# A graph layer with a mixture of experts: expert steps in multiples of 16 rows, and another list of steps

## The chip, the cores and the metric

The kernel runs on one core of a Trainium2 chip. The metric is the device time of one launch, the median over several runs: 1311.78 us before the change (three runs, 1311.54 to 1311.91). TensorE multiplies, VectorE (DVE) and ScalarE (ACT) work on vectors, GpSimd (POOL) issues the indirect transfers, and SyncE (SP) issues nearly all other transfers.

## The reference

For 6250 nodes of 256 features and 106250 edges (100000 random ones and a loop per node, sorted by target), the reference computes a graph convolution and then a feed-forward layer with 8 experts, of which each node uses its best two:

```python
deg = maximum(segment_sum(ones, dst), 1); norm = deg ** -0.5
y = norm * (layernorm(x) @ W.T + b)
x = x + norm * segment_sum(y[src], dst)                  # sum over the edges
g = layernorm(x)
p, idx = top_k(g @ Wg.T + bg, 2); p = softmax(p)
for e in range(8):                                       # W1[e]: 1024 x 256, W2[e]: 256 x 1024
    out += combine[..., e] * (relu(g @ W1[e].T + b1[e]) @ W2[e].T + b2[e])
x = x + out
```

All of it is float32. The kernel computes an expert only for the rows that chose it: 2 x 6250 = 12500 rows over the eight experts.

## The kernel before, in words

The kernel is one program with an order written out by hand. It has four parts.

**Start.** Node degrees are counted, the nodes are normalised, and a table with one row per node is written to memory (`ftable`).

**The stream.** The edges lie in 831 chunks of 128. For each chunk, called a slot here, POOL issues one indirect transfer that gathers 128 rows of the table (`gather`, L459), DVE makes a mask, and TensorE multiplies mask and rows into a window of sums (`add_up`, L473). The gather runs 6 slots ahead in the order of the program and has 24 buffers. When the edges of a tile of 128 nodes are all in, the tile goes through a chain of small tasks that are planned by slot: its sums are joined, multiplied by W (L566), normalised, scored, its two experts found, its rows sorted by expert (L698) and sent to a queue per expert in memory (`fhq`, L721, eight transfers on SP's queue).

**Expert steps.** The rows in the queues are worked off in steps. One step takes up to a fixed number of rows of one expert. `choose` (L730 and on) picks on DVE the expert with the most waiting rows at that moment. Then SP loads the expert's W1 (`load_first`, L773, 1152 KB), the rows (`load_rows`, L781) and W2 (`load_second`, L786, 1028 KB); each weight has three buffers, so W1 of a step is loaded when at most two steps ahead of it have not finished their up half, and W2 likewise by finished steps. TensorE works in pieces. An *up* piece (L814) computes 128 of the 1024 hidden values: two float32 matmuls, which the profile shows as four records, whose moving operand has as many columns as the step has rows. ACT applies bias and relu (L816). A *down* piece (L824) multiplies two of the eight blocks of hidden values by W2, for 128 rows of the step: again four records, with 256 columns. So a step has 8 up pieces, and 4 down pieces for each half of 128 rows. Up pieces of one step alternate with down pieces of the step before. When a half is complete, DVE adds the bias (L836) and SP writes the result to memory (`fyq`, L838).

How many rows a step has, and from which slot its choice may be made, is in the list STREAM (52 steps); nine further steps (TAIL) are chosen behind the stream, when all rows are sent. In every slot TensorE's order is filled by a credit: 1250 ns per slot, less 225 for the slot's own matmul and the planned tasks, and pieces are issued as long as credit is left:

```python
credit = min(credit + SLOT - CHUNK - busy.get(s, 0), SPARE)
while credit > 0:
    ...
    kind = next_piece(s)
    if not kind: break
    credit -= PIECES[ROWS_OF[of[kind == "down"]]][kind == "down"]
```

Pieces that are left when the slots run out follow one by one (the tail), together with the chains of the last tiles.

**End.** Each node's two results are read back by indirect transfers on POOL's queue (`read_back`, L907, 98 of them), weighed and added (L915), and the output is stored (L922). The list DONE says which tiles may be read back after which step: a pair (step, tile) means that all rows of tiles below `tile` lie in steps up to `step`. Before a group is read, `results` (L902) makes its addresses on DVE. If a tile's rows should lie in a later step than DONE says, or rows be left over, a flag is set, and a second, slower way of computing everything is entered (`any_order`).

Of the kernel before, what the change touches and what calls it, by code (L numbers as in the profile page):

```python
# [19 lines left out]
P = 128  # L20
N = 6250
NT = 49
# [12 lines left out]
CAP = 27 * FT  # L35
QR = NE * CAP
SLOTS = 64
STREAM = ((58, 128), (64, 128), (70, 128), (89, 128), (125, 256), (131, 256), (154, 256), (169, 256),
          (184, 256), (199, 256), (214, 256), (230, 256), (247, 256), (264, 256), (281, 256), (293, 256),
          (310, 256), (325, 256), (341, 256), (355, 256), (371, 256), (386, 256), (401, 256), (417, 256),  # L40
          (433, 256), (450, 256), (467, 256), (484, 256), (501, 256), (518, 256), (535, 256), (553, 256),
          (570, 256), (587, 256), (604, 256), (621, 256), (633, 256), (650, 256), (665, 128), (673, 256),
          (689, 256), (705, 256), (720, 256), (735, 128), (744, 256), (760, 256), (775, 256), (790, 256),
          (806, 256), (821, 128), (829, 128), (838, 128))
TAIL = (256, 256, 256, 256, 256, 256, 128, 128, 128)
ROWS_OF = [n for s, n in STREAM] + list(TAIL)
USUAL = len(ROWS_OF)
START = [P + sum(ROWS_OF[:step]) for step in range(USUAL + 1)]


# [1 line left out]
CHUNK = 225  # L52
SPARE = 2000
TASKS = dict(turn_sum=220, linear=890, rank=100, sort=430, inputs_turned=800, inputs_scored=1570)
PIECES = {FT: (915, 870), P: (600, 870)}
W1C = 2 * H + HB
W2C = HB * D + D

# [7 lines left out]
GROUP = 7  # L66
SHIFT = 1.0 / 16

DONE = ((36, 26), (38, 28), (40, 29), (41, 30), (42, 31), (43, 32), (46, 35), (49, 37), (50, 38), (51, 39),
        (52, 41), (55, 42), (57, 43), (58, 44), (59, 48), (USUAL - 1, NT))  # L70
LATER = 1 << 17
TURNED, PLACED, SORTED, SENT = 5, 17, 22, 24
LEAD = (13, 12)
# [73 lines left out]
def in_order(ctx: ExitStack, tc: tile.TileContext, g: Shared):  # L147
# [670 lines left out]
    def down(step, i, s):  # L818
        f = steps[step]
        a = i // 4  # L820
        if i % 4 == 0:
            f["py"] = psp.tile([P, D], F32, name="py")
        for b in (2 * (i % 4), 2 * (i % 4) + 1):
            nc.tensor.matmul(f["py"], f["hid"][:, b, a * P:(a + 1) * P], f["w2"][:, b * D:(b + 1) * D],  # L824
                             start=(b == 0), stop=(b == HB - 1))
        if i % 4 == 3:
            plan_at(s + 1, leave, step, a, f["py"], f["w2"])
        if i == 4 * ROWS_OF[step] // P - 1:
            del steps[step]


    def leave(step, a, py, w2):

        nonlocal gone
        y = work.tile([P, D], F32, name="y", bufs=4)
        nc.vector.tensor_add(y, py, w2[:, HB * D:])  # L836
        r0 = START[step] + a * P
        w = nc.sync.dma_start(yq[r0:r0 + P, :], y)  # L838
        free_order(w, reads, "results are written once, and read once written")
        writes.append((step, w))  # L840
        if a == ROWS_OF[step] // P - 1:
            gone += 1


# [91 lines left out]
    def next_piece(s):  # L936

        nonlocal curu, curd, done, upped, was
        was = next_kind(s)
        if was == "up":  # L940
            up(upped, curu)
            curu += 1
            if curu == HB:
                upped, curu = upped + 1, 0
        if was == "down":
            down(done, curd, s)
            curd += 1
            if curd == 4 * ROWS_OF[done] // P:
                done, curd = done + 1, 0
        return was  # L950

    with tc.manual_schedule():
        with rowp as rowpool:
# [5 lines left out]
            for s in range(NC):  # L959
# [8 lines left out]
                while credit > 0:  # L968
                    of = upped, done
                    kind = next_piece(s)  # L970
                    if not kind:
                        break
                    credit -= PIECES[ROWS_OF[of[kind == "down"]]][kind == "down"]
        with tc.tile_pool(name="ftail", bufs=2) as pool:
            s = NC
            pend = []
# [568 lines left out]
```

## Time and profile before

| | |
|---|---|
| median of the runs | 1311.78 us |
| the profiled execution | 1585.69 us |
| its span, first to last instruction | 1583.8 us |
| mean granted TensorE clock | 0.896 |
| first and last matmul of a slot (L473) | 76.9 and 1365.3 us |
| read-backs | 98 x 0.965 us on POOL |
| last TensorE piece ends, last instruction ends | about 1561.7 and 1583.8 us |

The profile is of one execution, recorded by the hardware, and it takes 274 us longer than the runs that are timed. A row of its groups names line, engine, operation and operands, then the number of instructions, the busy time and the mean duration of one, then the idle time ahead of it and what ended it. The duration of a matmul holds the time in which its results drain; the next one has begun by then, so the price of a piece is the distance from start to start. The row of stages gives, for a stretch of time, the busy time of each engine, the granted clock, the share of the DMA engines that was busy, and the rate of bytes.

### The profile page before, as it was taken

What the parts mean: (1) busy time and instruction counts of PE and PEld (TensorE: products, weight loads), DVE (VectorE), ACT (ScalarE), POOL (GpSimd) and SP (SyncE); (2) the same over time, 40 slices, a digit from 0 to 9 for tenths busy, and PEclk for the clock granted to TensorE, in tenths of its full rate; (3) what the DMA queues carried; (4) which work ended last, traced back from release to release, by engine and by line L of the source; (5) the groups of instructions that cost most, each with busy time, mean ns of one, the idle gap of its engine ahead of it and who ended that gap; (6) DMA issues with size and microseconds to landing.
All of it is one profiled execution on the core that took longest, in us unless ns stands there. A gap on an engine that the chain in (4) does not pass through costs nothing.

```text
span 1583.8 us, 24462 instructions
## 1 busy us (share of the span) xinstructions
PE 1255.9 (79%) x6400; PEld 953.5 (60%) x6400; DVE 980.3 (62%) x5472; ACT 397.4 (25%) x949; POOL 904.2 (57%) x975
## 2 busy tenths in 40 slices
PE   5239678479889888898988787888889888777894
PEld 5226566256666566666666565666666666665783
DVE  8611665565667676776766676767766676574632
ACT  3502222122222222222222222232222222221221
POOL 2166656556666566565666666656666664236633
PEclk9955678789999999899899999999999999888997
DMA  7633485577767676767767776767867767678863
GB/s 230 209 93 91 117 273 167 133 232 224 234 207 222 205 246 219 232 183 241 216 216 217 226 228 206 229 202 219 270 216 239 245 210 231 197 232 304 312 229 119
DMA packets 160925, 337.35 MB, mean 213 GB/s; under 512 B 26900, under 2 KB 106344, under 8 KB 145160
## 3 DMA queue, kind: packets, MB, share of 16 engines
q1 hardware_dynamic: 114348, 207.57, 37.7%
q0 software_dynamic: 46176, 127.59, 28.9%
q8 instruction: 52, 0.85, 0.2%
q14 instruction: 97, 0.79, 0.2%
q10 hardware_dynamic: 252, 0.53, 0.1%
HBM read 280.44 MB, written 55.16 MB: 212 GB/s over the span
## 4 chain that ended last, share of the span: by engine, by line
PE 60%; DVE 17%; issue 10%; another core or an unknown queue 6%; ACT 2%; DMA 2%; POOL 1%; SPq 1%; ACTq 0%; DVEq 0%; POOLq 0%
PE ph L814 22%; PE py L824 18%; PE ps L473 10%; PE pt L566 3%; PE ph L516 2%; DVE mask L466 2%; PE px L698 2%; PE count L291 1%; ACT hid L816 1%; DVE rolled L533 1%; PE px L505 1%; DVE rs L595 1%; DVE rolled L536 1%; DVE scr L750 1%
## 5 line engine op out<-in xcount | busy, mean ns | idle before, releaser
L459 POOL DMA_INDIRECT rows<-ftable,src x831 | 789.4, 950 | 508.6 <-PE ps L473 187.4
L814 PE MATMUL ph<-xT,w 128*128 128x256 f32 (+1 forms) x1952 | 515.4, 392 | 115.0 <-issue 65.3
L814 PEld LDWEIGHTS ph<-xT,w 128*128 128x128 f32 x1952 | 366.0, 203 | 236.9 <-issue 107.6
L824 PE MATMUL py<-w,hid 128*128 128x256 f32 x1760 | 468.9, 393 | 0.0
L816 ACT ACTIVATE hid<-ph,w 128x256 f32<-128x256 f32 (+1 forms) x488 | 216.9, 451 | 791.5 <-PE ps L473 260.6
L824 PEld LDWEIGHTS py<-w,hid 128*128 128x128 f32 x1760 | 340.8, 197 | 76.9 <-issue 2.7
L473 PE MATMUL ps<-rows,mask 128*128 128x512 f16 x831 | 327.4, 409 | 38.8 <-DMA rows<-ftable,src 28.3
L466 DVE TENSOR_SCALAR mask<-col_b,rel 128x128 f16<-128x128 bf16 x831 | 199.1, 266 | 32.5 <-issue 11.6
L907 POOL DMA_INDIRECT yb<-fyq,rowat x98 | 94.6, 965 | 113.7 <-DMA fyq<-y 54.0
L473 PEld LDWEIGHTS <-mask 128*128 128x128 f16 x831 | 88.1, 107 | 71.8 <-issue 32.2
L836 DVE TENSOR_TENSOR y<-py,w 128x256 f32<-128x256 f32 x110 | 46.4, 422 | 134.4 <-PE py L824 61.8
L533 DVE SCALAR_TENSOR_TENSOR rolled<-rolled,keep,ps 128x256 f32<-128x256 f32 x149 | 70.7, 474 | 44.7 <-PE ps L473 34.5
L573 DVE SCALAR_TENSOR_TENSOR xr<-pt,norm,xr 128x256 f32<-128x256 f32 x49 | 23.7, 483 | 118.8 <-PE ps L473 55.2
L548 ACT ACTIVATE whole<-rolled 32x256 f32<-32x256 f32 (+2 forms) x156 | 63.8, 409 | 59.8 <-DVE rolled L536 26.6
L516 PE MATMUL ph<-wg,turned 128*128 128x8 f32 x196 | 39.9, 332 | 48.2 <-issue 26.5
L516 PEld LDWEIGHTS ph<-wg,turned 128*128 128x128 f32 x196 | 38.7, 291 | 62.4 <-issue 33.7
L536 DVE TENSOR_TENSOR rolled<-ps,rolled 128x256 f32<-128x256 f32 x150 | 63.6, 424 | 15.8 <-DVE rolled L533 7.2
L566 PE MATMUL pt<-gw,uT 128*128 128x264 f32 x196 | 58.3, 424 | 18.3 <-issue 7.2
L698 PE MATMUL px<-slots,h2s 128*128 128x256 f16 x196 | 33.1, 297 | 37.2 <-DVE slots L686 20.4
L915 DVE SCALAR_TENSOR_TENSOR xr<-yb,prob,xr 128x256 f32<-128x256 f32 x98 | 46.0, 482 | 25.3 <-DMA yb<-fyq,rowat 23.2
L566 PEld LDWEIGHTS pt<-gw,uT 128*128 128x128 f32 x196 | 40.0, 209 | 34.6 <-issue 19.8
L698 PEld LDWEIGHTS <-h2s 128*128 128x128 f16 x196 | 20.5, 105 | 54.1 <-issue 42.4
(184 smaller groups left out, 1127.1 us busy)
## 6 DMA issues: line engine op xcount, KB each, us to landing
w<-in_W SPq DMA_DIRECT2D x61, 1152.0 KB
w<-in_W SPq DMA_DIRECT2D x61, 1028.0 KB
fhq<-ordered SPq DMA_DIRECT2D x392, 64.0 KB
fyq<-y SPq DMA_DIRECT2D x110, 128.0 KB
rows<-ftable,src POOLq DMA_INDIRECT x831
xT<-fhq SPq DMA_DIRECT2D x49, 256.0 KB
out<-xr POOLq DMA_DIRECT2D x11, 512.0 KB
xr<-in_x SPq DMA_DIRECT2D x6, 896.0 KB
```

The costliest lines, as they stand in the source:

```text
L459: nc.gpsimd.indirect_dma_start(out=rows[c], out_offset=None, in_=table[:, :], in_offset=bass.IndirectOffsetOnAxis(ap=g.src[:, c:c + 1], ax ...
L466: nc.vector.tensor_scalar(masks[c], g.col_b[:, r:r + P], g.rel[:, c:c + 1], None, op0=OP.is_equal)
L473: nc.tensor.matmul(sums[w], masks.pop(c), rows.pop(c), start=(c == chunks[0]), stop=(c == chunks[-1]))
L516: nc.tensor.matmul(px[:, t - t0], xT[:, k, (t - t0) * P:(t - t0 + 1) * P], wg[:, k, :], start=(k == 0), stop=(k == 1))
L533: nc.vector.scalar_tensor_tensor(new, rolled, keeps[kept[w]], ps[:, 0:D], op0=OP.mult, op1=OP.add)
L536: nc.vector.tensor_add(new, ps[:, D:2 * D], new)
L566: nc.tensor.matmul(pl, uT[:, k, :], gw[:, k, :], start=(k == 0), stop=(k == 1))
L698: nc.tensor.matmul(r.px[:, k, :], h2s[r.t][:, i, k * P:(k + 1) * P], slots[r.t], start=(i == 0), stop=(i == 1))
L814: nc.tensor.matmul(ph[:, :n], w1[:, k * H + b * P:k * H + (b + 1) * P], f["xT"][:, :n, k], start=(k == 0), stop=(k == 1))
L816: nc.scalar.activation(f["hid"][:, b, :n], ph[:, :n], AF.Relu, bias=w1[:, 2 * H + b:2 * H + b + 1])
L824: nc.tensor.matmul(f["py"], f["hid"][:, b, a * P:(a + 1) * P], f["w2"][:, b * D:(b + 1) * D], start=(b == 0), stop=(b == HB - 1))
L907: r = nc.gpsimd.indirect_dma_start(out=yb, out_offset=None, in_=yq[0:START[upto + 1], :], in_offset=bass.IndirectOffsetOnAxis(ap=where[:, ...
```

## The change

Steps may have any multiple of 16 rows up to 256. A half of a step that isn't full has `m` rows instead of 128, in the matmuls of the down pieces, in the bias add and in the write. An up piece is priced by its columns, 29 ns for eight of them and at least 300 ns, instead of by a table with two entries: 928 instead of 915 ns for 256 rows, 464 instead of 600 for 128. The list STREAM has 53 entries instead of 52: five steps of 128 rows and one of 208, then 37 of 256, then ten of 128 rows from slot 762 to 844. TAIL has eight steps of falling size instead of nine. DONE is another list, for the new steps. The lines of the diff:

```diff
--- before.py
+++ after.py
@@ -35,16 +35,17 @@
 CAP = 27 * FT
 QR = NE * CAP
 SLOTS = 64
-STREAM = ((58, 128), (64, 128), (70, 128), (89, 128), (125, 256), (131, 256), (154, 256), (169, 256),
-          (184, 256), (199, 256), (214, 256), (230, 256), (247, 256), (264, 256), (281, 256), (293, 256),
-          (310, 256), (325, 256), (341, 256), (355, 256), (371, 256), (386, 256), (401, 256), (417, 256),
-          (433, 256), (450, 256), (467, 256), (484, 256), (501, 256), (518, 256), (535, 256), (553, 256),
-          (570, 256), (587, 256), (604, 256), (621, 256), (633, 256), (650, 256), (665, 128), (673, 256),
-          (689, 256), (705, 256), (720, 256), (735, 128), (744, 256), (760, 256), (775, 256), (790, 256),
-          (806, 256), (821, 128), (829, 128), (838, 128))
-TAIL = (256, 256, 256, 256, 256, 256, 128, 128, 128)
+STREAM = ((74, 128), (91, 128), (99, 128), (108, 128), (118, 128), (126, 208), (175, 256), (183, 256),
+          (206, 256), (222, 256), (237, 256), (253, 256), (268, 256), (284, 256), (300, 256), (316, 256),
+          (332, 256), (348, 256), (365, 256), (380, 256), (395, 256), (411, 256), (427, 256), (450, 256),
+          (467, 256), (480, 256), (497, 256), (513, 256), (529, 256), (545, 256), (560, 256), (575, 256),
+          (591, 256), (607, 256), (623, 256), (638, 256), (655, 256), (672, 256), (686, 256), (702, 256),
+          (719, 256), (737, 256), (754, 256), (762, 128), (771, 128), (784, 128), (796, 128), (804, 128),
+          (812, 128), (820, 128), (828, 128), (836, 128), (844, 128))
+TAIL = (256, 224, 208, 208, 176, 160, 144, 128)
 ROWS_OF = [n for s, n in STREAM] + list(TAIL)
 USUAL = len(ROWS_OF)
+HALVES = [-(-n // P) for n in ROWS_OF]
 START = [P + sum(ROWS_OF[:step]) for step in range(USUAL + 1)]
 
 
@@ -52,7 +53,7 @@
 CHUNK = 225
 SPARE = 2000
 TASKS = dict(turn_sum=220, linear=890, rank=100, sort=430, inputs_turned=800, inputs_scored=1570)
-PIECES = {FT: (915, 870), P: (600, 870)}
+DOWN = 870
 W1C = 2 * H + HB
 W2C = HB * D + D
 
@@ -66,8 +67,8 @@
 GROUP = 7
 SHIFT = 1.0 / 16
 
-DONE = ((36, 26), (38, 28), (40, 29), (41, 30), (42, 31), (43, 32), (46, 35), (49, 37), (50, 38), (51, 39),
-        (52, 41), (55, 42), (57, 43), (58, 44), (59, 48), (USUAL - 1, NT))
+DONE = ((34, 25), (36, 27), (38, 28), (39, 29), (40, 30), (41, 31), (42, 32), (43, 34), (44, 35), (45, 36),
+        (47, 37), (49, 38), (50, 39), (53, 40), (55, 41), (56, 42), (58, 43), (59, 44), (USUAL - 1, NT))
 LATER = 1 << 17
 TURNED, PLACED, SORTED, SENT = 5, 17, 22, 24
 LEAD = (13, 12)
@@ -820,12 +821,13 @@
         a = i // 4
         if i % 4 == 0:
             f["py"] = psp.tile([P, D], F32, name="py")
+        m = min(P, ROWS_OF[step] - a * P)
         for b in (2 * (i % 4), 2 * (i % 4) + 1):
-            nc.tensor.matmul(f["py"], f["hid"][:, b, a * P:(a + 1) * P], f["w2"][:, b * D:(b + 1) * D],
+            nc.tensor.matmul(f["py"][:m], f["hid"][:, b, a * P:a * P + m], f["w2"][:, b * D:(b + 1) * D],
                              start=(b == 0), stop=(b == HB - 1))
         if i % 4 == 3:
             plan_at(s + 1, leave, step, a, f["py"], f["w2"])
-        if i == 4 * ROWS_OF[step] // P - 1:
+        if i == 4 * HALVES[step] - 1:
             del steps[step]
 
 
@@ -833,12 +835,13 @@
 
         nonlocal gone
         y = work.tile([P, D], F32, name="y", bufs=4)
-        nc.vector.tensor_add(y, py, w2[:, HB * D:])
+        m = min(P, ROWS_OF[step] - a * P)
+        nc.vector.tensor_add(y[:m], py[:m], w2[:m, HB * D:])
         r0 = START[step] + a * P
-        w = nc.sync.dma_start(yq[r0:r0 + P, :], y)
+        w = nc.sync.dma_start(yq[r0:r0 + m, :], y[:m])
         free_order(w, reads, "results are written once, and read once written")
         writes.append((step, w))
-        if a == ROWS_OF[step] // P - 1:
+        if a == HALVES[step] - 1:
             gone += 1
 
 
@@ -945,7 +948,7 @@
         if was == "down":
             down(done, curd, s)
             curd += 1
-            if curd == 4 * ROWS_OF[done] // P:
+            if curd == 4 * HALVES[done]:
                 done, curd = done + 1, 0
         return was
 
@@ -970,7 +973,7 @@
                     kind = next_piece(s)
                     if not kind:
                         break
-                    credit -= PIECES[ROWS_OF[of[kind == "down"]]][kind == "down"]
+                    credit -= DOWN if kind == "down" else max(300, 29 * ROWS_OF[of[0]] // 8)
         with tc.tile_pool(name="ftail", bufs=2) as pool:
             s = NC
             pend = []
```

## The prediction

> **What bounds the kernel now.** I read the page's busy shares first, then the groups of instructions by shape, then busy time by stage, then the timeline of the last 50 us. The profiled execution took 1585.69 us for a span of 1583.8; the median of the runs is 1311.78, so the profiled one is 274 us longer, and all sums below need a word on what carries over. The page:
>
> ```profile
> span 1583.8 us, 24462 instructions
> PE 1255.9 (79%) x6400; PEld 953.5 (60%) x6400; DVE 980.3 (62%) x5472; ACT 397.4 (25%) x949; POOL 904.2 (57%) x975
> ...
> q1 hardware_dynamic: 114348, 207.57, 37.7%
> q0 software_dynamic: 46176, 127.59, 28.9%
> ```
>
> TensorE is the busiest, and 57% for POOL looks harmless. The timeline of POOL at the start of the stream says otherwise: 831 row gathers in one queue, each 0.95 us and then 0.30 us of its own issue, so 1.25 us is the least a slot of the stream can take, and 831 x 1.25 = 1039 us the least for all.
>
> ```profile
> 90.64 0.95 POOL L459 DMA_INDIRECT rows<-ftable,src  x1 [0.30 <-issue]
> 91.89 0.94 POOL L459 DMA_INDIRECT rows<-ftable,src  x1 [0.30 <-issue]
> ```
>
> In the profile the stream runs from 76.9 to 1365.3 us, 1.55 us per slot, TensorE-paced with many short gaps put down to issue. The median run cannot look like that: take from 1311.78 the 76.9 before the first slot and, behind the stream, at least the 138 us of TensorE work worked out below and 22 us of end, and 1075 us are left, 1.29 per slot; with more gaps in the tail it comes down to the floor, 1039. So in the median run the stream stands at 1.25 to 1.29 us per slot, close to POOL's floor. Microseconds of dense TensorE work, of gathers and of the end I carry over unscaled; the gaps of the profile I do not.
>
> Behind the stream (from 1365) there are no gathers of that kind, and TensorE sets the time. By stage (columns: busy of PE, PEld, DVE, ACT, POOL, then granted clock, DMA share, GB/s):
>
> ```profile
> 1365.00:1419.00 54.00, 37.53 (x186) 30.93 (x185) 35.79 (x212) 11.93 (x33) 23.72 (x25) 0.79 0.67 209
> 1419.00:1457.00 38.00, 25.52 (x91) 19.05 (x90) 18.53 (x92) 6.57 (x15) 21.52 (x23) 0.81 0.93 350
> 1457.00:1562.00 105.00, 98.60 (x468) 83.47 (x467) 44.42 (x177) 26.10 (x61) 50.71 (x53) 0.95 0.67 232
> 1562.00:1584.00 22.00, 0.19 (x2) 0.09 (x2) 6.22 (x20) 0.00 (x0) 7.49 (x8) 0.61 0.37 111
> ```
>
> First 54 us in which the last tiles' chains leave gaps, then 38 us in which the weights of several steps arrive together (DMA share 0.93), then 105 us of solid TensorE, then 22 us of end with TensorE done.
>
> The price of a piece is read from start to start in the solid stretch, since the duration of a matmul holds its drain:
>
> ```profile
> 1525.96 0.86 PEld L814 LDWEIGHTS ph<-xT,w 128*128 128x128 f32 x4
> 1526.85 0.85 PEld L824 LDWEIGHTS py<-w,hid 128*128 128x128 f32 x4
> 1527.72 0.86 PEld L814 LDWEIGHTS ph<-xT,w 128*128 128x128 f32 x4
> ...
> 1533.24 0.62 PE L814 MATMUL ph<-xT,w 128*128 128x128 f32 x4
> ...
> 1534.56 0.62 PE L814 MATMUL ph<-xT,w 128*128 128x128 f32 x4
> ```
>
> A pair of up (256 columns) and down takes 1.76 us: 0.90 for the up piece, 0.87 for the down piece. With 128 columns a pair takes 1.32, so that up piece is 0.45. Both are 3.5 ns per column: an up piece of n rows costs n x 3.5 ns, a down piece 0.87 whatever its rows are, because its moving operand is w2 with 256 columns.
>
> **The change part by part.** I replayed the static plan of both versions and counted pieces (counts, no times).
>
> *All steps.* Both lists have 61 steps, so 61 loads of W1 and W2 either way. Rows computed go from 14080 to 13104: 976 x 8 x 3.5 ns = 27 us less up work. Half-steps go from 110 to 106: 16 down pieces x 0.87 = 14 us less. 41 us less TensorE work in all; what matters is where. Counted on the reference's routing, both lists take up all 12500 rows, so the second way of computing isn't entered.
>
> *Behind the stream.* Before: 49 up pieces of 256, 48 of 128 and 80 down: 44.1 + 21.6 + 69.6 = 135 us (138 with the last tiles' own matmuls). After: 40 up of 128, 8 each of 256, 224, 176, 160 and 144, 16 of 208, and 77 down: 18.0 + 7.2 + 6.3 + 4.9 + 4.5 + 4.0 + 11.7 + 67.0 = 124 us. That is 12 us less; 3 of them (17 against 14 us) stand ahead of slot 857, where the profile shows gaps anyway (the 54 us row). So 9 to 12, and I take -10.
>
> *In the stream.* The other 29 us. In a slot full of pieces both versions issue up to the same credit of 1.25 us; what changes is how many slots are full. Slots in which credit is left and nothing can be issued go from 138 to 188, most of them new between 153 and 193. If the gathers pace every slot the saving is hidden: 0. If TensorE paced all, it would be 29. A full slot is about 1.23 us at full clock by the piece prices and 0.216 for the gather's matmul, and 1.29 at the 0.95 granted in the dense stretches, 0.04 above the gather: 50 slots x 0.04 = 2 us, with something more where an idle slot works off a backlog. I take -3.
>
> Here a rule of the Trainium skill speaks against the change. TensorE: Matmul & The Clock Gate, Part 1, says that an idle TensorE falls to half its clock and needs a busy window of about 3.4 us to come back. The trace has it: granted 0.57 and 0.54 between 80 and 160 us, where pieces are few. In the new idle slots TensorE has 0.216 and some 0.17 of tile work; at half clock 0.77 us, still under the gather's 1.25. By the rule one more return to full clock costs 1.7 us once; by the slot's sum nothing, and I enter nothing.
>
> *Weights at the stream's end.* Ten 128-row steps mean 2180 KB of weights every 8 to 11 slots instead of every 16. First W1 issues between slots 774 and 823: five steps instead of three. Five steps x 2.5 MB (weights, xT, y) + 49 gathers x 0.131 + three sends x 0.52 = 20.5 MB in 49 x 1.25 = 61 us, 335 GB/s; before 266. The row of the crunch moved 350 at share 0.93, so 376 at full: 89%, no wait. By the shares of the two queues (127.59 MB in 28.9% and 207.57 in 37.7% of the span, so 279 and 348 GB/s when full) it is 23 + 40 = 63 us of transfer in 61: 2 us late. DMA: Bandwidth & Descriptors, Specifications, gives about 358 GB/s of HBM per core: 94%. I take +1, from 0 to +3 for bytes alone; what late weights could do to the queue of pieces is a rival below.
>
> *Start of the tail.* A step of the tail is chosen only when all rows are sent, slot 857 in both. Before, the first of them has 11 pieces (6.6 us) between its W1 issue and its use; TensorE stood 2.84 us for it:
>
> ```profile
> 1425.02 1.14 PE L814 MATMUL ph<-xT,w 128*128 128x256 f32 x4 [2.84 <-DMA xT<-fhq]
> ```
>
> After, 17 pieces (9.7 us), and one step fewer loads in that moment. I take -3 (0 to -10, since other gaps of those 38 us may shrink too).
>
> *The end.* Of the read-backs before, eight wait for the last but one step and two for the last; they start at 1558.47 and the two at 1571.71, and the last TensorE piece ends at 1561.7, 22 us ahead of the end. The new list of bounds leaves five tiles instead of one to the last step: ten gathers behind `results`. Two for tile 43 start at about the end of TensorE, are added about 5 us later, and then ten at 1.25 run one after another in POOL's queue: the last is issued 5.4 + 9 x 1.25 = 17 us after TensorE's end, where before it was 11.3 (1572.95). Nothing covers it: +5.5.
>
> Edits at nothing: the loads, transfers and adds of fewer rows are shorter, never longer, and lie beside TensorE; 61 choices cost DVE the same.
>
> Sum: -10 - 3 + 1 - 3 + 5.5 = -9.5 us: 1576.2 for the profiled execution by this sum, and 1302 for the median.
>
> **The rivals.** *TensorE paces the stream in the median run too.* For it: 79% busy, and in the profile POOL waits 187 us for L473. Against it: the 1.25 to 1.29 us per slot above. Then most of the 29 us count: -6.5 - 20 = -26, 1285.
>
> *Slower: late weights in slots 774 to 862.* Each of ten short steps has W1 issued 8 to 12 us of pieces ahead of use, through one SP queue in which sends and y writes wait too, and TensorE takes pieces in order, so the gathers' matmuls and the last tile's chain queue behind a piece without weights. For it: SP was held for 11.35 us by one tile's sends at 1369.57, and DMA ran at 0.93. It decides from 1.0 us of lateness per step (ten steps eat the 9.5 us); at 2 us it is +10: 1322. Against it: 89 to 94% by bytes, and triple-buffered weights.
>
> *No change:* the tail is set by transfers (about 25 MB of weights, 13 MB of read-backs, 6 MB of output), so 10 us less TensorE only becomes wait and the end's +5.5 cancels the rest: 1312. Against it: the solid 105 us at share 0.67.
>
> **How the numbers follow.** The sum as forecast (1296 to 1308) 0.47; TensorE-paced stream (1274 to 1296) 0.23; late weights (1315 to 1330) 0.22; no change 0.08. Within 0.2% is 2.6 us, about what a measurement of this kernel can tell. Faster 0.70, same 0.08, slower 0.22. Predicted 1302. The range of 8 in 10 leaves a third of each outer case: 1284 to 1323.
>
> **What would show it.** Up pieces of 208, 176, 160 at 3.5 ns per column, or less saved if weight loads bind; POOL idle less before L459 in slots 153 to 193; DMA share above 0.85 in the last 100 us of the stream, with or without waits of L814 and L824 there; the first tail step without its 2.84 us; ten gathers in a row at the end, and 27 us instead of 22 behind the last TensorE piece. The forecast is wrong if the stream shortens by more than 10 us or the short steps wait for w.

## The result, and the profile after

The changed kernel takes 1324.66 us (median of 4 runs, 1321.03 to 1326.21), the kernel before 1311.66 (4 runs, 1308.83 to 1311.91): ratio 1.010, 95% interval 1.0073 to 1.0127. It is 13 us slower. The forecast was 1302, faster with a chance of 0.70, and a range of 1284 to 1323: the sign is wrong, and the range is missed by 1.7 us.

On some chips every execution of every kernel here took some 250 us longer, and its trace, like the one shown with the prediction, holds stops of each engine for which no releaser is named (called "the stops" below), so each kernel is set against the kernel before on the same chip, and times inside traces are compared where both have the stops or both lack them.

The profiled execution of the changed kernel took 1326.21 us for a span of 1324.3 and has no such stops, so its page and the page shown before cannot be subtracted. The page of the changed kernel (first lines, and two groups of instructions):

```profile
span 1324.3 us, 24330 instructions
PE 1163.0 (88%) x6336; PEld 902.6 (68%) x6336; DVE 977.9 (74%) x5474; ACT 402.0 (30%) x949; POOL 904.8 (68%) x974
...
L910 POOL DMA_INDIRECT yb<-fyq,rowat x98 | 95.9, 979 | 81.0 <-DVE rowat L905 22.8
L918 DVE SCALAR_TENSOR_TENSOR xr<-yb,prob,xr 128x256 f32<-128x256 f32 x98 | 46.2, 482 | 55.5 <-DMA yb<-fyq,rowat 54.6
```

POOL's share of busy time is again a number that sounds harmless. The two last lines are those that the prediction left out of its sum for the part behind the stream: 98 read-backs of expert results (L910, 0.98 us each, 0.30 of issue between them), and their 98 additions on VectorE, which stood idle 54.6 us for those rows.

By stage (columns: busy time of PE, PEld, DVE, ACT, POOL; granted clock, DMA share, GB/s): the end of the stream in two parts, the last tiles' chains, the steps behind them, and the end.

```profile
1050.00:1090.00 40.00, 39.99 (x221) 33.29 (x220) 29.91 (x185) 14.32 (x37) 30.49 (x32) 0.97 0.93 313
1090.00:1128.00 38.00, 35.48 (x214) 29.71 (x213) 28.61 (x192) 13.82 (x39) 19.87 (x21) 0.96 0.97 352
1128.00:1181.00 53.00, 40.10 (x220) 33.93 (x219) 44.99 (x254) 14.55 (x41) 26.90 (x28) 0.88 0.85 279
1181.00:1296.00 115.00, 106.73 (x508) 86.73 (x508) 51.33 (x211) 26.73 (x64) 65.33 (x68) 0.95 0.77 279
1296.00:1324.00 28.00, 0.55 (x4) 0.09 (x2) 7.43 (x23) 0.00 (x0) 11.74 (x12) 0.54 0.36 106
```

Two rows matter. From 1181 to 1296 TensorE is busy for 106.7 of 115 us at a clock of 0.95, in a stretch that the prediction called solid. From 1296 on there are 28 us with TensorE done, 22 before.

What did TensorE and VectorE wait for behind the stream (1128 to 1297)? The tables of waits give total us, times, and the longest. VectorE, the largest:

```profile
DVE xr L918 <- DMA yb<-fyq,rowat: 41.5, 25, 6.0
```

TensorE:

```profile
PE py L826 <- DVE y L839: 8.3, 3, 4.0
PE ph L815 <- DMA xT<-fhq: 4.2, 1, 4.2
PE pt L635 <- DVE chose L621: 3.7, 2, 3.3
PE pt L555 <- DVE spot L651: 3.6, 1, 3.6
```

TensorE stands 8.3 us for a `py` buffer (where a half of a step collects its results) that VectorE has yet to empty. VectorE stands 41.5 us for read-back rows. One of the three cases, as a timeline (start, duration, engine, line, then idle time ahead and its releaser):

```profile
1251.43 0.48 DVE L918 SCALAR_TENSOR_TENSOR xr<-yb,prob,xr 128x256 f32<-128x256 f32 x1 [3.28 <-DMA yb<-fyq,rowat]
1252.04 0.94 POOL L910 DMA_INDIRECT yb<-fyq,rowat  x1 [0.30 <-DVE xr L918]
...
1253.29 0.95 POOL L910 DMA_INDIRECT yb<-fyq,rowat  x1 [0.30 <-issue]
1253.43 0.48 DVE L918 SCALAR_TENSOR_TENSOR xr<-yb,prob,xr 128x256 f32<-128x256 f32 x1 [1.52 <-DMA yb<-fyq,rowat]
...
1253.90 0.42 DVE L839 TENSOR_TENSOR y<-py,w 128x256 f32<-128x256 f32 x1
...
1254.38 2.07 PE L826 MATMUL py<-w,hid 128*128 128x256 f32 x4 [4.03 <-DVE y L839]
```

VectorE has these instructions in the order of the program. The addition L918 stands at its head until the row lands; behind it waits L839, which empties `py`; with both `py` buffers held, the matmul L826 waits 4.03 us. POOL issues one read-back behind another with only its 0.30 us of issue between: at this moment the queue of read-backs is full.

The same stretch in slices of 5 us shows the cost (columns as above):

```profile
1181.00:1186.00 5.00, 5.00 (x13) 3.93 (x14) 4.51 (x27) 0.47 (x1) 3.85 (x4) 0.52 1.02 384
...
1226.00:1231.00 5.00, 3.45 (x17) 2.89 (x18) 4.58 (x29) 0.59 (x2) 3.97 (x4) 1.00 0.83 227
1231.00:1236.00 5.00, 3.16 (x16) 2.38 (x14) 2.56 (x9) 1.30 (x3) 3.89 (x4) 1.00 1.00 414
1236.00:1241.00 5.00, 4.46 (x15) 3.91 (x16) 3.00 (x9) 0.41 (x1) 3.92 (x5) 0.66 0.99 360
...
1251.00:1256.00 5.00, 1.62 (x4) 1.35 (x5) 1.86 (x5) 0.00 (x0) 3.78 (x5) 0.80 0.92 346
1256.00:1261.00 5.00, 5.00 (x26) 4.62 (x25) 3.24 (x9) 1.18 (x3) 2.96 (x4) 0.85 0.45 142
```

Read POOL's column first: 3.8 us busy of 5 sounds like 76%, but four instructions of 0.95 and four issues of 0.30 are 5.0 us. It is full, or nearly so, in all but one slice from 1186 to 1256, those left out here included. It was not full all the way: between 1149 and 1180 it stood 16.6 us for VectorE, once 9.64 us ahead of a store of finished output, and behind 1260 it stands again. Then PE's: 8 us missing between 1226 and 1256. Then the clock: after a stop it is 0.52, 0.66, 0.80, 0.85 for a slice; (1 - clock) x 5 us summed over these four is 5.9 us more.

### The profile page after: what moved, and what is told of

It reads as the page before. It is cut to its first block, busy times and chain, and to the rows that moved or that the text cites. A ratio compares the mean times of both kernels' runs of the same rounds, so it can differ in the third digit from the quotient of the medians.

```text
span 1324.3 us, 24330 instructions
## 1 busy us (share of the span) xinstructions
PE 1163.0 (88%) x6336; PEld 902.6 (68%) x6336; DVE 977.9 (74%) x5474; ACT 402.0 (30%) x949; POOL 904.8 (68%) x974
## 3 DMA queue, kind: packets, MB, share of 16 engines
q0 software_dynamic: 46032, 127.07, 32.8%
## 5 line engine op out<-in xcount | busy, mean ns | idle before, releaser
L460 POOL DMA_INDIRECT rows<-ftable,src x831 | 790.2, 951 | 286.6 <-issue 104.6
L815 PE MATMUL ph<-xT,w 128*128 128x256 f32 (+6 forms) x1952 | 457.5, 364 | 14.7 <-DMA xT<-fhq 13.6
L826 PE MATMUL py<-w,hid 128*128 128x256 f32 (+4 forms) x1696 | 437.7, 384 | 8.3 <-DVE y L839 8.3
L815 PEld LDWEIGHTS ph<-xT,w 128*128 128x128 f32 x1952 | 347.7, 196 | 114.3 <-issue 32.3
L474 PE MATMUL ps<-rows,mask 128*128 128x512 f16 x831 | 322.3, 406 | 67.9 <-DMA rows<-ftable,src 38.7
L817 ACT ACTIVATE hid<-ph,w 128x256 f32<-128x256 f32 (+6 forms) x488 | 214.2, 440 | 531.1 <-PE ph L815 453.7
L826 PEld LDWEIGHTS py<-w,hid 128*128 128x128 f32 (+4 forms) x1696 | 312.9, 188 | 79.2 <-DVE y L839 9.2
L910 POOL DMA_INDIRECT yb<-fyq,rowat x98 | 95.9, 979 | 81.0 <-DVE rowat L905 22.8
L918 DVE SCALAR_TENSOR_TENSOR xr<-yb,prob,xr 128x256 f32<-128x256 f32 x98 | 46.2, 482 | 55.5 <-DMA yb<-fyq,rowat 54.6
L839 DVE TENSOR_TENSOR y<-py,w 128x256 f32<-128x256 f32 (+5 forms) x106 | 44.5, 420 | 53.1 <-PE py L826 52.3
L638 ACT ACTIVATE h2s<-h 128x256 f16<-128x256 f32 x49 | 20.3, 415 | 126.3 <-DVE h L629 126.1
L567 PEld LDWEIGHTS pt<-gw,uT 128*128 128x128 f32 x196 | 39.2, 201 | 16.6 <-issue 5.9
L596 DVE TENSOR_SCALAR rs<-ry,rv 128x1 f32<-128x1 f32 x147 | 39.7, 270 | 1.8
L292 PE MATMUL count<-oh,ol 128*16 128x8 bf16 (+2 forms) x898 | 30.3, 176 | 12.2 <-DVE oh L278 9.0
```

Of the source, the lines that this page charges most:

```text
L460: nc.gpsimd.indirect_dma_start(out=rows[c], out_offset=None, in_=table[:, :], in_offset=bass.IndirectOffsetOnAxis(ap=g.src[:, c:c + 1], ax ...
L474: nc.tensor.matmul(sums[w], masks.pop(c), rows.pop(c), start=(c == chunks[0]), stop=(c == chunks[-1]))
L567: nc.tensor.matmul(pl, uT[:, k, :], gw[:, k, :], start=(k == 0), stop=(k == 1))
L815: nc.tensor.matmul(ph[:, :n], w1[:, k * H + b * P:k * H + (b + 1) * P], f["xT"][:, :n, k], start=(k == 0), stop=(k == 1))
L817: nc.scalar.activation(f["hid"][:, b, :n], ph[:, :n], AF.Relu, bias=w1[:, 2 * H + b:2 * H + b + 1])
L826: nc.tensor.matmul(f["py"][:m], f["hid"][:, b, a * P:a * P + m], f["w2"][:, b * D:(b + 1) * D], start=(b == 0), stop=(b == HB - 1))
```

## The experiments

**Half the read-backs.** My theory after the result was that POOL's queue of read-backs, and not TensorE, sets the time behind the stream. To test it, half of it is taken away: the second transfer of each tile is left out and its first row is added twice, so VectorE's work stays.

```
     def read_back(pool, where, t, j, upto=USUAL - 1):
-        yb = pool.tile([P, D], F32, name="yb", bufs=12)
+        if j:
+            return t, j, rows_of[t]
+        yb = rows_of[t] = pool.tile([P, D], F32, name="yb", bufs=12)
```

The edit was made to the changed kernel twice, and to the kernel before twice.

> After, with the transfer of every second read-back left out (the row read for the first expert is added for the second as well; 49 of 98 transfers, all adds stay). Theory R: 10 us or more faster than after, of which some 6 at the end, where five of the ten last read-backs fall away. Theory T: 6 us for the end and some more for 5 MB less. If only the 6 us of the end: the read-backs inside the tail cost nothing.

> The kernel before, with the transfer of every second read-back left out, as in half_read_backs. By the pieces' times, 84 read-backs are asked for in the first 93 us of pieces here and in 82 us in after, and POOL needs 117: TensorE is held 10 us less here. If so, before gains 8 to 12 us where after gained 20.6 (6 of these at the end). If the read-backs hold both alike, it gains as much as after, and the stream or the weights cost the difference.

> The kernel before without the transfer of every second read-back, beside the next run on one chip. If the read-backs hold TensorE less in before than in after: 0.990 to 0.994 of before in executions without stalls (8 to 12 us), against 20.6 us for after; with stalls 0.977 as measured. If they hold both alike: 0.984.

> After, likewise. If the read-backs and the end make the difference of 1.2%: within 0.4% of before_half_2 on the same chip. If the stream or the weights make it: 0.8 to 1.2% slower than before_half_2.

Without the stops, the changed kernel went to 1307.66 (the changed kernel itself 1328.3 on that chip) and 1305.33; ratios to the kernel before 0.9965 (0.9932 to 0.9997) and 0.998 (0.9965 to 0.9994). The kernel before went from 1308.66 to 1300.85: 0.9949 (0.993 to 0.9969). So the same edit is worth 20.6 us to the changed kernel (19.3 against its first median) and 7.8 to the one before. About 6 of the 20.6 and 4 of the 7.8 are the end, where fewer read-backs are left (28.0 to 22.2 us, 22.0 to 18.0). With half the read-backs the two kernels are 4.5 us apart; whole they are 13 apart by the first medians and 17.5 on the chip of the first of these runs. With the stops the edit gave the kernel before 0.9768 (0.9715 to 0.9821), 35 to 39 us; I use that one no further than to say that the tail is bound in the same place there.

Stages of the kernel before with half the read-backs:

```profile
1050.00:1090.00 40.00, 39.92 (x190) 30.78 (x189) 29.74 (x174) 11.50 (x28) 30.25 (x33) 1.00 0.85 268
1090.00:1128.00 38.00, 37.43 (x179) 29.13 (x178) 27.65 (x175) 11.21 (x26) 23.36 (x25) 1.00 0.88 285
1128.00:1167.00 39.00, 30.00 (x178) 26.12 (x176) 35.17 (x209) 11.26 (x31) 10.51 (x12) 0.95 0.80 260
1167.00:1279.00 112.00, 111.55 (x540) 96.02 (x540) 58.03 (x242) 31.60 (x72) 40.92 (x44) 0.99 0.77 282
1279.00:1296.00 17.00, 0.19 (x2) 0.09 (x2) 5.80 (x20) 0.00 (x0) 2.44 (x3) 0.62 0.34 105
```

Of the changed kernel with half the read-backs, from the stream's end:

```profile
1128.00:1178.00 50.00, 39.95 (x218) 33.76 (x217) 41.86 (x248) 14.55 (x41) 13.45 (x14) 0.90 0.80 269
1178.00:1279.00 101.00, 100.59 (x508) 82.38 (x506) 53.71 (x218) 26.73 (x64) 37.47 (x39) 1.00 0.75 277
1279.00:1301.00 22.00, 0.19 (x2) 0.09 (x2) 7.17 (x23) 0.00 (x0) 6.01 (x6) 0.54 0.32 99
```

And what its TensorE waited for from 1128 to 1280, the largest:

```profile
PE pt L555 <- DVE spot L651: 3.6, 1, 3.6
PE pt L635 <- DVE chose L621: 3.5, 2, 3.3
PE ph L815 <- DMA xT<-fhq: 1.6, 1, 1.6
```

The wait for `py` is gone. The same 508 matmul instructions that took 115 us now take 101, at full clock: 14 us, of which 8.3 were the wait for `py` and 106.73 - 100.59 = 6.1 the lowered clock. Beside the 112 us of the kernel before stands the predicted saving of TensorE's work: from the first tail step to the last piece 111.6 us there and 101.2 here, 10.4 less. The saving is real; in the whole changed kernel the same stretch takes 116.4 and 115.5 us in its two traces. The edit takes away turns in POOL's queue (65 to 37 us busy) and bytes (279 GB/s x 115 us = 32 MB, then 277 x 101 = 28), so it can't tell the two apart; the run without weight transfers below bears on that.

**More TensorE work in the tail.** If TensorE set the tail, longer pieces would cost their time. Here the eight tail steps have 416 rows more, 416 x 8 x 3.5 ns = 11.6 us of up pieces, with the same number of pieces:

```
-TAIL = (256, 224, 208, 208, 176, 160, 144, 128)
+TAIL = (256, 256, 256, 256, 256, 256, 256, 128)
```

> After, with a tail of seven steps of 256 rows and one of 128: the same steps of the same experts, 416 rows more computed, 416 x 28 ns = 11.6 us more TensorE work. Theory P: 11.6 us slower than after. Theories T and R: within 4 us of after, since the tail waits for something else.

1328.73 us beside 1328.3 of the changed kernel on the same chip: ratio to the kernel before 1.0134 (1.0102 to 1.0166), beside 1.012 (1.0084 to 1.0156). 11.6 us of work cost 0.4, with some 4 us of uncertainty on either ratio. Its tail, and with it where the work went:

```profile
1179.00:1296.00 117.00, 112.97 (x508) 95.70 (x507) 50.72 (x208) 29.43 (x64) 64.62 (x68) 0.96 0.77 279
```

The stretch is 117 us instead of 115, with TensorE busy 6.2 us more; its wait for `py` fell from 8.3 to 4.0 us. The shrinking of the tail steps behind the new stream, the core of the change, bought nothing that can be measured.

The companion of these two on the same chip was the changed kernel once more:

> The changed kernel itself, on the chip of the other three, as their reference. 1.010 to 1.015 of before, whether executions have the stalls or not.

**Tail without weight transfers.** Steps 55 to 60 use the weights of step 54:

```
         f = steps[step]
+        if 55 <= step <= 60:
+            f["w1"] = held["w1"]
+            return
         f["w1"] = held["w1"] = wts.tile([P, W1C], F32, name="w1")
```

and the same for `w2`.

> After, with the W1 and W2 transfers of steps 55 to 60 left out (they compute with step 54's weights). Theory T: the tail is set by its transfers, not by TensorE, so that TensorE work taken from it comes back as waiting; these six steps hold 13 MB of about 45 MB in the tail. Then 10 us or more faster than after. Theory R: it is set by the read-backs, which pass POOL's queue at 1.25 us each and then DVE's queue: less than 4 us. Theory P, TensorE's pieces set it: no change.

1320.58 us, 7.7 less than the changed kernel beside it; ratio to the kernel before 1.0077 (1.005 to 1.0104). DMA share behind 1181 fell from 0.77 to 0.54, VectorE's wait for read-back rows from 41.5 to 32.8 us, TensorE's for `py` from 8.3 to 3.3, but one wait for xT was 6.0. POOL's busy time is the same (64.7 and 65.3 us). So transfers have a share in the wait, by this run 5 us of the 8.3 for `py`: VectorE waits less for rows when no weights move beside them. But bytes alone don't explain the read-backs: six steps of weights are 13 MB and gave 7.7 us, 49 read-backs are 6.4 MB and gave 20.6, or about 15 without the end.

**Old stream, short tail.** This takes the stream of the kernel before, whose ten steps at the end aren't short, with even less TensorE work behind it: 608 rows and one step less, 17 us of up pieces by the piece prices. The number of down pieces stays, since both tails have 15 halves.

```
-TAIL = (256, 256, 256, 256, 256, 256, 128, 128, 128)
+TAIL = (208, 192, 192, 176, 160, 144, 144, 96)
```

with the bounds of the read-backs as before, but ending in (58, 44) and the last step.

> The stream list of before with a tail of eight steps with just enough rows (208, 192, 192, 176, 160, 144, 144, 96) in place of nine, by the code of after: 60 steps, and 17 us less of up pieces behind the stream than before, five tiles read back behind the last step. If late weights of the ten short steps are the cause, this keeps the tail's gain without them: 1311.7 - 17 + 5 = 1300. If the tail doesn't give its TensorE work back (its transfers and read-backs set its time), 1311 to 1320.

> Once more: the stream of before with the tail of eight short steps. In the first try 1.0002 of before, where 12 us less was hoped for. Theory A: the tail's shorter pieces run into the read-backs here too, so 0.998 to 1.006 of before. Theory B: 0.99.

1.0002 (0.9977 to 1.0026) and 0.999 (0.9969 to 1.001), both on chips with the stops: no difference. The end grew by 5.7 us (27.7 and 27.8, 22.0 before), so the stretch from the last gather's matmul to the last TensorE piece shrank by about as much: 189.1 and 185.7 us, beside 191.1 and 190.0 of the kernel before in the same jobs. At most 5 of 17 us came through. With the kernel before once more on each of these chips:

> The kernel before, once more, for a trace: its profiled execution was 274 us longer than its timed runs, and after's is not (span 1324.3 against a median of 1324.66), so the two traces can't be laid side by side by stage. Expected: 1309 to 1312 us. If the slower end is as in the forecast, the end behind the last TensorE piece is 22 us here and 28 in after. If late weights cost the time, TensorE's waits for transfers between the gathers of the last 100 us of the stream and the first steps behind it are some 10 us fewer here than in after. If the stream itself is slower, the last gather's matmul ends earlier here than at 1128.5 us.

> The kernel before, for a trace that can be laid beside after's (the last one, like the first, was one of an execution with stalls all over, 1588.6 us). Expected where executions run without them: the last gather's matmul at the same time as in after, 1128 us, since both streams are held by the gathers; TensorE's end at about 1288 and 22 us of end, where after has 1296.4 and 28.

**The short steps without their weights.** For the rival of late weights, steps 43 to 52 computed with step 42's, in the manner of the edit above.

> After, with the W1 and W2 transfers of the ten short steps 43 to 52 left out (they compute with the weights that step 42 loaded; all else stays). It takes 22 MB out of the stretch in which after's DMA share is 0.95. If late weights are the cause: 14 us or more faster than after, at or below before's 1311. If the read-backs and the end are the cause: within 4 us of after's 1324.7, since that stretch's transfers don't touch them.

> Once more: after without the W1 and W2 transfers of steps 43 to 52. In the first try the executions had stalls all over and it was no faster than the others (1.0166 of before). Theory B: 1311 or less where after is 1324.7 (ratio to before 1.000 or below). Theory A: 1.007 or more of before.

1.0166 (1.0121 to 1.0212) and 1.0146 (1.0077 to 1.0215), on chips with the stops. The end of the stream of that kernel:

```profile
1337.00:1377.00 40.00, 36.23 (x212) 30.01 (x213) 28.24 (x191) 13.66 (x39) 4.72 (x5) 0.96 0.20 57
```

With the DMA share down to 0.20, TensorE is busy 36.2 us of 40, much as in the changed kernel at 0.97 (35.5 of 38), and the ratio is not below the changed kernel's 1.010 to 1.012. No gain shows, but the unedited changed kernel wasn't run on those two chips, and with stops in the stream a late transfer may be covered. It speaks against the rival and doesn't exclude it where the stops are missing.

**The end made early.** The last two bounds of the plan merged, so that the tiles up to 47 may be read back from step 58 on, and only the last tile waits for the last step; what rows steps 59 and 60 hold for tiles 43 to 47 is left out.

```
-            plan = list(DONE)
+            plan = list(DONE[:-3]) + [(58, 48), (USUAL - 1, NT)]
```

> After, with tiles 43 to 47 read back behind step 58 instead of behind steps 59 and 60, so that only two read-backs are left for the end (rows of those tiles that lie in steps 59 and 60 are left out of the sum). It prices the end. If the ten read-backs in a row are worth what the forecast says, the 28 us behind the last TensorE piece become about 16: 12 us faster than after, 1312. If read-backs only move from the end into a tail that is held by transfers and by DVE, less than 5 us.

1.0153 (1.0091 to 1.0215), with the stops. The end fell from 28 to 15.6 us as it should, but the tail before it took 205.7 us, beside 191.1 of the kernel before in the same job: the eight read-backs came off the end and into the tail. Moved, not saved, as far as this shows: the changed kernel itself never ran on a chip with the stops.

**Later additions on VectorE.** If the additions stand at VectorE's head because they are issued too early, issuing them later should free it. The distance between asking for a row and adding it goes from 8 pieces to 12, with more buffers, and then to 28:

```
-        yb = pool.tile([P, D], F32, name="yb", bufs=12)
+        yb = pool.tile([P, D], F32, name="yb", bufs=30)
...
-                if pend and (gone == USUAL or len(pend) > 10 or s >= pend[0][0] + 8):
+                if pend and (gone == USUAL or len(pend) > 28 or s >= pend[0][0] + 28):
```

> After, but a read-back row is added 12 pieces behind its issue instead of 8 (16 buffers instead of 12). Theory A: pieces of smaller steps are shorter (0.8 instead of 0.885 us in the mean), so 3 read-backs per 4 pieces are asked for every 1.07 us where POOL's queue takes 1.25, the rows come ever later, DVE waits for them in its queue (54.6 us in after), the result adds of the experts stand behind, and TensorE waits for their PSUM (8.3 us, at half clock afterwards). Then 8 us or more faster than after, 1316 where after is 1324.7. Theory B, late weights of ten short steps: no change, within 3 us of after.

> After, but a read-back row is added 28 pieces behind its issue (30 buffers) instead of 8. All transfers stay. If the adds that wait in DVE's queue hold the experts' results and so TensorE: 8 to 15 us faster than after, its tail near the 151.5 us that half the read-backs gave. If the transfers themselves are in the way (DMA share 0.9): less than 3 us.

> The stream of before, the tail of eight short steps, and adds 28 pieces behind the issue. If the adds were what hid the tail's saving, 10 to 20 us faster than before: 1292 to 1300. If POOL's queue is the bound even so (84 read-backs take 117 us behind the stream, and 42 us of pieces and the end follow), about before's 1311.

All on chips with the stops, so beside 1.010 and 1.012 of the changed kernel from other chips: 1.011 (1.0042 to 1.0177) at 12, 1.0172 (1.0111 to 1.0233) at 28, and the old stream with the short tail at 28 1.0122 (1.0062 to 1.0181), where without that edit it was 0.999 to 1.0002. The kernel before beside the last two:

> The kernel before, for a trace beside after's in an execution without stalls. If POOL's read-backs pace the tail in both, TensorE's end stands 158 to 162 us behind the last gather's matmul (after: 168), though TensorE has 12 us more to do; then 22 us of end (after: 28).

No gain, and at 28 a loss for which the trace offers a cause. POOL's largest wait from 1380 to 1600 of the changed kernel at 28:

```profile
POOL out L925 <- DVE xr L918: 51.5, 4, 39.0
```

The stores of finished output (L925) are issued from POOL's queue as well, each behind the additions of its tiles. With late additions the stores stand at POOL's head for 51.5 us, and the read-backs behind them aren't issued. So this edit turned one wait into another and doesn't test the theory that it was made for. A kernel with both the late additions and the stores on another queue wasn't run.

## Why the prediction was wrong

By its own steps, in the runs without stops. The traces of both kernels with half the read-backs give the split, because there is no such trace of the kernel before whole: its last gather's matmul is at 1123.3 us (changed: 1127.9), its first tail step 43.7 us later (49.7), the end of the last TensorE piece 111.6 us after that (101.2), and the end 18.0 us (22.2). The sum of the differences is 4.6 + 6.0 - 10.4 + 4.2 = 4.4, and the two medians differ by 4.5. The rest is the read-backs: the other half of them costs the changed kernel 19.3 us (1324.66 to 1305.33) and the one before 7.8 (1308.66 to 1300.85), 11.5 more; 4.5 + 11.5 is the 16 between 1324.66 and 1308.66. These are one trace of each kernel, and the 1324.66 is from another job than the other three medians; between jobs without the stops, medians of one kernel differ by 2 to 4 us here.

*Behind the stream, -10: the step that failed.* The count of pieces was right. Up pieces of 208 columns cost what the prediction said, by the starts of two in a row:

```profile
1208.82 0.90 PE L815 MATMUL ph<-xT,w 128*128 128x208 f32 x4
1209.55 1.02 PE L826 MATMUL py<-w,hid 128*128 128x256 f32 x4
```

0.73 us for 208 columns is 3.5 ns each. One price was too low: a down piece is not 0.87 us whatever its rows are. In halves of 48, 32 and 16 rows it takes 0.99, 0.98 and 0.97 us, and the up pieces beside it take 0.1 to 0.2 more than 3.5 ns per column; in halves of 80 and 96 rows nothing is added. Up pieces of 160 columns in the changed kernel with half the read-backs, first beside a half of 128 rows, then beside one of 48:

```profile
1239.01 0.73 PE L815 MATMUL ph<-xT,w 128*128 128x160 f32 x4
1239.57 1.02 PE L826 MATMUL py<-w,hid 128*128 128x256 f32 x4
1240.43 0.73 PE L815 MATMUL ph<-xT,w 128*128 128x160 f32 x4
...
1246.93 0.83 PE L815 MATMUL ph<-xT,w 128*128 128x160 f32 x4
1247.69 1.06 PE L826 MATMUL py<-w,hid 128*48 128x256 f32 x4
1248.69 0.83 PE L815 MATMUL ph<-xT,w 128*128 128x160 f32 x4
```

A pair takes 1.42 us, then 1.76. Three steps have such a half, with four pairs each: some 3.7 us that the sum didn't have. Even so, 10 us appear (111.6 to 101.2) as soon as half the read-backs are gone. With all of them the changed kernel takes 115.5 us there. The kernel before would take about 115 (an estimate: 111.6 and the 7.8 - 4.0 us that half the read-backs save it ahead of the end), so the forecast 10 became nothing. The sentence that was wrong is "TensorE sets the time", taken from a TensorE busy 98.6 of 105 us. The prediction found that POOL's 57% hid a full queue in the stream, and did not ask the same of the same engine behind it. That sum was to be had from its own numbers. The code asks for a read-back on a fixed count of pieces, so shorter pieces ask faster: in the plan, 80 read-backs (tiles 0 to 39) are asked for within 92 us of pieces before, by the piece prices, and within 82 after. POOL needs 80 x 1.25 = 100 us for them, without the output stores between them. By this estimate, which leaves out TensorE's own gaps, it was short by 8 us and became short by 18. The TensorE work that was saved was time in which the queue was to be worked off.

What is shown: with half the read-backs the loss in this stretch is gone, and TensorE's own work can grow by 11.6 us for 0.4. Not shown apart is how much of it is turns in POOL's queue and how much the later landing of rows beside the weights (7.7 us came back without those). What is read from traces and not shown by a run of its own is the path from POOL to TensorE, over the order on VectorE and the two `py` buffers.

*Start of the tail, -3: wrong.* The first tail step of the changed kernel stands longer for its rows than the 2.84 us of the trace before, not less:

```profile
1180.84 2.04 PE L815 MATMUL ph<-xT,w 128*128 128x256 f32 x4 [4.25 <-DMA xT<-fhq]
```

It starts 52.3 us after the last gather's matmul. With half the read-backs it starts after 49.7, against 43.7 in the kernel before with half of them, whose TensorE waits in this stretch are:

```profile
PE ph L814 <- DMA xT<-fhq: 4.1, 1, 4.1
PE pt L554 <- DVE spot L650: 2.0, 1, 2.0
PE pt L634 <- DVE chose L620: 0.9, 1, 0.9
```

Between these two the wait for rows does fall as forecast, 4.1 to 1.6, and with all read-backs that is lost again (4.25). But the waits of the last tiles' chains for `spot` and `chose` grow from 2.9 to 7.1 us, and the granted clock of the stretch falls from 0.96 to 0.90, about 3 us. By the plan the pieces ahead of the first tail step are 26 us of work in both kernels, so more work isn't the reason. The prediction counted pieces between issue and use as if they ran without gaps; why VectorE is later with the chains stays open.

*Weights at the stream's end, +1, and stream, -3: about +5 together.* The forecast DMA share came: 0.93 and 0.97 where the kernel before with half the read-backs has 0.85 and 0.88. The last 30 slots take 1128.5 - 1085.9 = 42.6 us in the changed kernel (40.7 with half its read-backs), and 37.7 in that kernel before. The size is uncertain: in the six traces without the stops that have the changed stream, those slots take 39.7 to 42.8 us and the last gather's matmul stands at 1126.2 to 1133.3 us, and there is only the one such trace of the stream before. Each of the six waits 0.6 to 3.4 us for rows of a step in these slots, the kernel before not at all, and none waits for weights. The wait in the changed kernel:

```profile
1120.08 2.43 PE L815 MATMUL ph<-xT,w 128*128 128x128 f32 x12 [2.43 <-DMA xT<-fhq]
```

The rival of late weights gave 1322 us, and 1324.66 is near it, but by the wrong road: it wanted ten steps late by 2 us each in the stream, and the whole stream lost about 5. Whether those 5 come from transfers of weights, which move beside the rows, stays open, as told above. The 358 GB/s that the prediction took as the most a core can get is not the most here: slices of 5 us moved up to 414. The gain of 3 from fuller slots did not come: 1.267 us per slot over the stream here, 1.261 in the kernel before with half the read-backs, both next to the 1.25 of the gathers, so the gathers pace it as forecast and TensorE's saving there is hidden.

*The end, +5.5: right.* 22.0 us became 28.0 (18.0 and 22.2 with half the read-backs). These two may be compared across the stops: the end is 21.7 to 22.2 us in all four traces of the kernel before, and 27.3 to 28.0 with the changed list in traces with and without them. The last TensorE piece, two read-backs for tile 43, then ten, then the store:

```profile
1296.40 0.42 DVE L839 TENSOR_TENSOR y<-py,w 128x256 f32<-128x256 f32 x1 [3.69 <-PE py L826]
...
1302.08 0.94 POOL L910 DMA_INDIRECT yb<-fyq,rowat  x1 [2.72 <-DVE late L1031]
...
1313.73 0.95 POOL L910 DMA_INDIRECT yb<-fyq,rowat  x1 [0.30 <-issue]
...
1317.51 0.50 ACTq L927 DMA_DIRECT2D out<-xr  x1
```

The last read-back is issued 17.3 us after TensorE's end; 17 was worked out.

*The clock, entered as nothing.* In the sparse slots 153 to 193 of the stream that holds: granted 0.69 in the changed kernel, and POOL's gathers still only 0.30 us apart. (Of the two rows that the prediction named for lack of pieces, 120 to 160 us isn't one: TensorE was busy 37 of 40 us there at 0.54.) In the tail it doesn't hold: the rule of the Trainium skill (TensorE: Matmul & The Clock Gate, Part 1, idle halves the clock) shows as 0.52 behind the 4.25 us wait, and the four lowered slices cost about 6 us, more than its 1.7 once, since TensorE stopped several times. Behind the first tail step it isn't a cause of its own: without the waits it was 1.00.

*The rivals.* That transfers set the tail ("no change", 0.08) was nearest in mechanism: it named read-backs, weights and output, and that saved TensorE time would only become wait. It was priced to a draw because it counted the read-backs' 13 MB and not their 98 turns in one queue, and gave no cost to the same turns being asked for sooner. TensorE pacing the stream is out by the 1.267 us per slot.

## What to carry to other kernels

Count every engine's queue per stage, with its issue time, before calling a stage bound by the one that looks busiest: a DMA issuer 76% busy can be full. Where one engine's work is paced by another's count of instructions, shortening those instructions speeds up the asking and not the answering, and a saving comes back as waits (here 10 us saved in the tail, and 11.5 more lost to read-backs, the end included). A share of 93 to 97% for TensorE doesn't show that it sets the time; making its work longer, and seeing whether the time follows, does.

## What the runs showed of the hardware that was not expected

On three of the five chips used for the experiments, all executions had the stops, and the kernel before has a median of 1565.11 to 1584.66 us; on the two others none had, and it has 1310.8 and 1308.66. The duration of a gather (0.95 us) and the medians of DMA packets (159 ns for 4096 bytes, 27 for 512) are the same. In the 13 traces with the stops TensorE stands 19 to 28 times for more than 1.5 us with no releaser named (behind the first 80 us), in the seven without not once. Each chip was used once, so the chip and the hour can't be told apart, and the cause was not found. With half the read-backs the kernel before gains in both cases, but 35 to 39 us with the stops and 7.8 without.

An indirect DMA of 128 rows costs its queue on POOL 0.95 us and 0.30 of issue, in the stream (L460) and for most read-backs in the tail (L910, 0.94 to 1.18). A store in that queue that waits for VectorE holds back every read-back behind it, 51.5 us in four waits of one kernel.

A matmul piece whose stationary operand has 16, 32 or 48 columns (a down piece of so few rows) took 0.97 to 0.99 us where one of 80, 96 or 128 took 0.86, and slowed the 128-column pieces on either side, each by 0.1 on the side where they touch it. By these numbers, down pieces that take 128 columns of hidden values for such a half too, as in the kernel before, would avoid it; that wasn't run.
